# Gated cross-attention with RMS norm: another order for the last outer product and for the norms of the last four tiles

## The chip, the cores and the metric

The kernel runs on one core of a Trainium2 chip. The core has five engines that run side by side, each with its own list of instructions in a fixed order: TensorE (PE, matmuls into PSUM; PEld is its loading of weights), VectorE (DVE), ScalarE (ACT), GpSimd (POOL) and SyncE (SP), which here only issues DMAs. Engines wait for each other by semaphores. The metric is the time of one execution in microseconds (us), measured on the device.

## The reference

Eight batches of 1024 rows (`hidden_states`, the input x), 1024 wide, attend to a memory of 64 rows of 512 per batch (the context), which is projected first. All is fp32.

```
memory_proj = einsum('bme,de->bmd', memory, W_mem)
scores = einsum('bnd,bmd->bnm', hidden_states, memory_proj) / sqrt(D)
attn = softmax(scores)
memory_context = einsum('bnm,bmd->bnd', attn, memory_proj)
gate_input = concatenate([hidden_states, memory_context], -1)
gate = sigmoid(einsum('bnf,df->bnd', gate_input, W_gate) + b_gate)
fused = hidden_states + gate * memory_context
out = fused * rsqrt(mean(fused**2) + 1e-6) * norm_w
```

## The kernel before

**Tiles and stages.** A setup projects the memory and multiplies the projection with the second half of the gate's weights, so that what remains per row is x times the first half of `W_gate` (1024 x 1024) plus attention times that product. Then 16 "quads" follow, each of 4 tiles of 128 rows (`QT` = 512, `NQ` = 16). The large product of a quad is done by a two-level Strassen-Winograd scheme: seven outer products (`ORDER`: 1, 6, 7, 5, 4, 2, 3), each of which is made of seven inner products named A, B, C, D, A, E, F, of 128 x 256 results in PSUM banks `kA` to `kF`. The last but one call of `outer_product` takes 8.16 us (its first matmul at 944.12 us, that of the next call at 952.28).

**One outer product.** `product` issues two matmuls (four records in the trace) and calls `step`, which first runs everything that falls due at this slot. VectorE forms the running sums `u2`, `u3`, `u4` from B, C and D (lines with `u<-u,kB` and so on). GpSimd adds them into the blocks of the output (`pre`, three additions of 128x256). VectorE adds the finished banks (`fin`). GpSimd also forms the left sums of the next outer product (`inner_s`, tiles `l`), in two parts of two additions.

**The last four outer products of a quad** also complete blocks of the output: they have an `ext`, and between the second product into A and product E they issue attention's part, sixteen records of 64-row matmuls. Half of them go into two banks `pc` (attention times projected memory, for two tiles of 128x512), and the other half add attention's share of the gate to `kA`, `kF`, `kE` and `kD`. The pairs go in the order `pc`/A, `pc`/F, then, in the second `pc` bank, `pc`/E, `pc`/D. A bank may be written only after VectorE has read what it held: two `pc` banks take turns, and `kD` must have been read by `u<-u,kD`.

**After an outer product with `ext`**: `sigmoid` on ScalarE (in place, tile `gate`), `gated` on VectorE (times `pc`), then the residual x, the mean of squares, the norm and the store. In the last quad (`q` = `NQ`-1) x has been loaded into tile `xl` (`load_last`), and VectorE adds it (`last_gated`, line 714 and on); ScalarE squares with an accumulator (line 724) and folds in the other half's sum (line 727) or takes the square root (`last_root`, line 736); VectorE takes the reciprocal and scales by it and by `nw_sb`, the norm's weights (`last_norm`, lines 745 and 749); SP stores 128x512 at a time. Outer product 4 completes tiles 2 and 3 ("row 1"), outer product 3 tiles 0 and 1 ("row 0"), the first halves of both having been done before. In a row, `d` is the odd tile and `c` the even one; `d` goes first. ScalarE must load a table of functions when it goes from sigmoid to square root (`sqrt_table`, line 756, does so ahead of the need).

**Order.** Every instruction is pinned to its place in the program, so an engine runs its list in the order of the calls. What falls due is set by slots: `at(slot + n, fn, ...)`. For the last two outer products before:

```
            when = (4, 5, 7, 9, 11, 12) if o == 4 else (2, 4, 5, 6, 7, 8)
            at(slot + when[0], last_root, d)
            at(slot + when[1], last_root, c)
            for w_, (t, h_) in zip(when[2:], ((d, 0), (d, 1), (c, 0), (c, 1))):
                at(slot + w_, last_norm, t, h_)
```

Of the kernel before, what the change touches and what calls it, by code (L numbers as in the profile page):

```python
# [9 lines left out]
AF = mybir.ActivationFunctionType  # L10
ALU = mybir.AluOpType
# [4 lines left out]
P = 128  # L16
# [4 lines left out]
def tile_gated_cross_attention_rmsnorm(  # L21
# [42 lines left out]
    nc = tc.nc  # L64
    B, N, D = x.shape
    M, E = mem.shape[1:]
    QT = 4 * P
    QPB = N // QT
    NQ = B * QPB
# [3 lines left out]
    H = 512  # L73
    C = 256
# [14 lines left out]
    pin = tc.keep_in_program_order  # L89

    def mm(o, lhsT, rhs, start, stop):
        pin(nc.tensor.matmul(o, lhsT, rhs, start=start, stop=stop, skip_group_check=True))  # L92

    def tt(eng, o, a, b, op):
        pin(eng.tensor_tensor(o, a, b, op))  # L95

    def load(o, i):
        pin(nc.sync.dma_start(o, i))

    def t4k(pool, shape, tag, name):  # L100
        return pool.tile(shape, F32, tag=tag, name=name)
# [34 lines left out]
    for k in range(KD):  # L136
        t = t4k(*((gpool, [P, D], "gate") if k < 7 else (apool, [P, D], "s4")), f"w2_{k}")
# [8 lines left out]
    nw_sb = const.tile([P, D], F32, name="nw_sb")  # L146
# [10 lines left out]
    R11, R21, R12, R22, T4, T1, T2 = range(7)  # L157
# [14 lines left out]
    def w_op(o, s):  # L172
        if s >= T4:
            return inner_t[o][:, s - T4, :, :]
        k, n = {R11: (0, 0), R21: (1, 0), R12: (0, 1), R22: (1, 1)}[s]
        return outer_b[o][:, 2 * k : 2 * k + 2, n * C : (n + 1) * C]
# [158 lines left out]
    A, S, L2, O = {}, {}, {}, {}  # L335
    sTs, attns, attnTs, scs, mps, mgs = {}, {}, {}, {}, {}, {}
    def where(q, t=0):
        return q // QPB, (q % QPB) * QT + t * P
# [30 lines left out]
    def left(q, o):  # L369

        return {
            1: lambda: A[q, 0, 0],
            2: lambda: A[q, 0, 1],
            3: lambda: S[q, 4],
            4: lambda: A[q, 1, 1],
            5: lambda: S[q, 1],
            6: lambda: S[q, 2],
            7: lambda: S[q, 3],
        }[o]()

    def quarters(l):
        return l[:, 0:2, 0:P], l[:, 2:4, 0:P], l[:, 0:2, P:], l[:, 2:4, P:]
# [214 lines left out]
    def at(slot, fn, *args):  # L597
        due.setdefault(slot, []).append(lambda: fn(*args))

    def mid(key, fn, *args):  # L600
        beside.setdefault(key, []).append(lambda: fn(*args))
# [47 lines left out]
    slot = 0  # L649

    def step():
        nonlocal slot
        for fn in due.pop(slot, ()):
            fn()

    def gated(q, t, h, pc):
        g = O[q, t][:, h * H : (h + 1) * H]
        tt(nc.vector, g, g, pc, ALU.mult)
# [46 lines left out]
    xl, halves = {}, {}  # L705
# [8 lines left out]
    def last_gated(t, h, pc):  # L714
        q = NQ - 1
        gated(q, t, h, pc)
        cols = slice(h * H, (h + 1) * H)
        g = O[q, t][:, cols]
        tt(nc.vector, g, g, xl[t][:, cols], ALU.add)
        if t not in halves:  # L720
            halves[t] = t4k(small, [P, 3], f"halves{t}", f"halves{t}"), h
        ss, first = halves[t]
        junk = t4k(small, [P, H], "junk", f"junk_{t}_{h}")
        pin(nc.scalar.activation(junk, g, AF.Square, accum_out=ss[:, h : h + 1]))
        if h == first:
            pin(
                nc.scalar.activation(
                    ss[:, 2:3], ss[:, h : h + 1], AF.Identity, bias=eps_sb, scale=1.0 / D
                )
            )  # L730

    def last_root(t):
        ss, first = halves[t]
        h = 1 - first
        pin(
            nc.scalar.activation(
                ss[:, 2:3], ss[:, h : h + 1], AF.Sqrt, bias=ss[:, 2:3], scale=1.0 / D
            )
        )

    def last_norm(t, h):
        b, n0 = where(NQ - 1, t)
        rstd = halves[t][0][:, 2:3]
        if h == 0:
            pin(nc.vector.reciprocal(rstd, rstd))
        cols = slice(h * H, (h + 1) * H)
        g = O[NQ - 1, t][:, cols]
        pin(
            nc.vector.scalar_tensor_tensor(g, g, rstd, nw_sb[:, cols], ALU.mult, ALU.mult)  # L749
        )  # L750
        load(out[b, n0 : n0 + P, cols], g)

    def sqrt_table():

        t = t4k(small, [P, 1], "warm", "warm")
        pin(nc.scalar.activation(t, eps_sb, AF.Sqrt))

    def outer_product(q, o, ext):

        nonlocal slot, banks  # L760
        l11, l12, l21, l22 = quarters(left(q, o))
        s1, s2, s3, s4 = (L2[q, o][:, i, :, :] for i in range(4))
        kb = {}

        def product(name, tag, lhsT, s, start=True):
            nonlocal slot
            step()
            if name not in kb:
                kb[name] = ps.tile([P, C], F32, tag=banks[tag], name=f"k{name}{q}_{o}")
            for k in range(2):  # L770
                mm(kb[name], lhsT[:, k, :], w_op(o, s)[:, k, :], start and k == 0, k == 1)
            slot += 1
# [24 lines left out]
        def pre(n, u):  # L797

            for dst, src in sums:
                if src is not None:  # L800
                    tt(nc.gpsimd, dst[n], src[n], u, ALU.add)

        def fin(n, name, u):
            for dst, src in sums:
                if src is not None:
                    tt(nc.vector, dst[n], (src if u is None else dst)[n], kb[name], ALU.add)
                elif u is not None:
                    tt(nc.vector, dst[n], u, kb[name], ALU.add)
                else:
                    pin(nc.scalar.copy(dst[n], kb[name]))  # L810

        ut = t4k(rot, [P, 4, C], "u", f"u{q}_{o}")
        p1, u2, u3, u4 = (ut[:, i, :] for i in range(4))
# [8 lines left out]
        product("D", 3, s1, T1)  # L822
        tt(nc.vector, u4, u2, kb["D"], ALU.add)
        pre(1, u4)
        product("A", 0, l12, R21, False)
        pcs = []
        if ext:
            row, h, g = ext
# [3 lines left out]
            for r, names in ((0, ("A", "F")), (1, ("E", "D"))):  # L832
                pc = ps_ctx.tile([P, H], F32, tag="ctx", name=f"pc{q}_{o}_{r}")
                for n in range(2):
                    cols = slice(h * H + n * C, h * H + (n + 1) * C)
# [14 lines left out]
                pcs.append(pc)  # L850
        for fn in beside.pop((q, o), ()):
            fn()
        fin(0, "A", None)
        fin(3, "D", u3)
        product("E", 4, l22, T4, not ext)
        fin(2, "E", u3)
        if ext:
            sigmoid(q, 2 * row + 1, h)
            last = q + 1 == NQ
            if last:  # L860
                at(slot + 2, last_gated, 2 * row + 1, h, pcs[1])
            else:
                at(slot + 1, gated, q, 2 * row + 1, h, pcs[1])
        product("F", 1, s4, R22, not ext)
        fin(1, "F", u4)
        if ext:
            sigmoid(q, 2 * row, h)
            if last:
                at(slot + 3, last_gated, 2 * row, h, pcs[0])
            else:  # L870
                at(slot + 2, gated, q, 2 * row, h, pcs[0])
        if o in (4, 3) and q + 1 == NQ:
            c, d = 2 * ext[0], 2 * ext[0] + 1
            if o == 3:
                sqrt_table()
            when = (4, 5, 7, 9, 11, 12) if o == 4 else (2, 4, 5, 6, 7, 8)
            at(slot + when[0], last_root, d)
            at(slot + when[1], last_root, c)
            for w_, (t, h_) in zip(when[2:], ((d, 0), (d, 1), (c, 0), (c, 1))):
                at(slot + w_, last_norm, t, h_)  # L880
        elif o in (4, 3):

            row = ext[0]
            c, d = 2 * row, 2 * row + 1
            for t in (d, c):
                at(slot + 5, residual, q, t)
            if row == 0:
                when = (17, 18, 23, 29, None, None)
            else:
                when = (17, 18, 23, 25, 29, 32)  # L890
            at(slot + when[0], square, q, c)
            at(slot + when[1], square, q, d)
            for w_, (t, h_) in zip(when[2:], ((c, 0), (c, 1), (d, 0), (d, 1))):
                if w_ is None:
                    mid((q + 1, 4), norm, q, t, h_)
                else:
                    at(slot + w_, norm, q, t, h_)
# [3 lines left out]
    for q in range(NQ):  # L901
        plan(q)
        for o, ext in ORDER:
            outer_product(q, o, ext)
    while due:
        slot = min(due)
# [27 lines left out]
```

## Time and profile before

| what | value |
|---|---|
| median of 4 runs | 972.51 us (972.19 to 972.57) |
| the profiled execution, its own time | 972.55 us |
| its span, first to last instruction | 970.7 us |
| granted TensorE clock, mean | 0.997 |
| TensorE busy | 959.2 us (99%) |
| VectorE busy | 818.7 us (84%) |
| GpSimd busy | 760.3 us (78%) |
| ScalarE busy | 328.6 us (34%) |
| end of the last matmul on the chain | 960.86 us |

In the order of time a line has the start in us, the duration in us, the engine, the line of the kernel, the operation, what is written and what is read, the shapes and the number of instructions merged; in brackets the idle time ahead of it and what ended that. The first duration of a merged line is the sum from first start to last end. Line 92 is the helper of all matmuls, line 95 that of all two-operand steps, line 98 that of all DMAs on SP's queue, so the names of tiles tell them apart. In the chain of work that ended last a line has start, duration and the engine whose work filled that time.

In the last 60 us the outer product of block 2 runs from 944.1 us, that of block 3 (the last) from 952.3 us.

### The profile page before, as it was taken

Reading aid. Unit: us, or ns where it says so; the run is one execution under the profiler, and the core shown is the slowest. Engines: PE = TensorE matmul, PEld = TensorE weight load, DVE = VectorE, ACT = ScalarE, POOL = GpSimd, SP = SyncE. Lnnn points to the kernel's source line nnn. Section 1 sums busy time; section 2 is a strip of 40 time slices with the busy share of each in tenths; the row PEclk is TensorE's granted clock in tenths of the full one; section 3 lists DMA queues with packets and bytes.
Section 4 is the critical chain, followed back from the end, with each engine's and each line's share of the span. In section 5 each row is a group of like instructions: output and inputs, shape, how many; then the busy total and the mean of one; then the engine's idle time right before and its main releaser. Section 6 shows DMA issues by size and latency. Waiting matters only on the chain.

```text
span 970.7 us, 14402 instructions
## 1 busy us (share of the span) xinstructions
PE 959.2 (99%) x4986; PEld 774.7 (80%) x4986; DVE 818.7 (84%) x1482; ACT 328.6 (34%) x604; POOL 760.3 (78%) x889
## 2 busy tenths in 40 slices
PE   9999999999999999999999999999999999999995
PEld 8646888788888888788888888888888878888884
DVE  6989879879797988979797988979797978979787
ACT  2000234161423334152433324152333425152345
POOL 4997878778786968878786978878687878878692
PEclk9999999999999999999999999999999999999998
DMA  9956673472919374482918365381918465391712
GB/s 375 273 142 160 101 133 96 117 166 73 177 66 167 107 134 103 107 176 64 186 65 158 104 137 114 93 190 53 197 67 147 114 129 122 87 196 48 189 68 86
DMA packets 70919, 128.32 MB, mean 132 GB/s; under 512 B 12352, under 2 KB 49216, under 8 KB 70592
## 3 DMA queue, kind: packets, MB, share of 16 engines
q1 hardware_dynamic: 61520, 93.34, 37.0%
q0 software_dynamic: 9184, 33.56, 18.9%
q8 instruction: 39, 0.64, 0.3%
q10 hardware_dynamic: 144, 0.52, 0.2%
q14 instruction: 32, 0.26, 0.1%
HBM read 87.56 MB, written 41.68 MB: 133 GB/s over the span
## 4 chain that ended last, share of the span: by engine, by line
PE 97%; DVE 1%; DMA 1%; ACT 0%; issue 0%; DVEq 0%
PE kA L92 20%; PE pc L92 12%; PE kE L92 11%; PE kD L92 10%; PE kF L92 10%; PE kC L92 10%; PE kB L92 10%; PE psT L92 6%; PE pg L92 5%; PE pm L92 3%; DMA memq<-in_mem 1%; PE sc L417 0%; PE pa L443 0%; DVE gate L749 0%; DVE it L95 0%
## 5 line engine op out<-in xcount | busy, mean ns | idle before, releaser
L95 POOL TENSOR_TENSOR gate<-gate,u 128x256 f32<-128x256 f32 x336 | 287.5, 887 | 107.3 <-DVE u L95 107.3
L662 ACT ACTIVATE gate<-gate 128x512 f32<-128x512 f32 x128 | 80.5, 631 | 305.5 <-DVE gate L95 304.8
L349 DVE STREAM_TRANSPOSE a<-xq 128x512 f32<-128x512 f32 x128 | 137.8, 1098 | 3.6 <-POOL w L95 3.6
L95 POOL TENSOR_TENSOR l<-a 128x256 f32<-128x256 f32 x128 | 122.4, 956 | 21.6 <-PE kA L92 21.6
L92 PE MATMUL pc<-mg,attnT 64*128 64x256 f32 x512 | 127.5, 389 | 0.0
L92 PE MATMUL kB<-it,l 128*128 128x256 f32 x448 | 115.1, 379 | 0.3 <-DVE gate L95 0.3
L92 PE MATMUL kD<-it,l 128*128 128x256 f32 x448 | 115.0, 379 | 0.0
L92 PEld LDWEIGHTS pc<-mg,attnT 64*128 64x128 f32 x512 | 90.6, 186 | 29.9 <-issue 21.2
L691 DVE SCALAR_TENSOR_TENSOR gate<-gate,ss,nw_sb 128x512 f32<-128x512 f32 x120 | 110.0, 926 | 1.1
L95 POOL TENSOR_TENSOR l<-s 128x256 f32<-128x256 f32 x96 | 77.8, 810 | 37.2 <-PE kF L92 30.4
L92 PE MATMUL kA<-w,a 128*128 128x256 f32 x384 | 98.6, 379 | 0.0
L92 PEld LDWEIGHTS kB<-it,l 128*128 128x128 f32 x448 | 85.1, 190 | 12.1 <-DVE gate L95 0.7
L92 PEld LDWEIGHTS kD<-it,l 128*128 128x128 f32 x448 | 85.2, 190 | 11.5
L95 DVE TENSOR_TENSOR gate<-gate,pc 128x512 f32<-128x512 f32 x128 | 86.6, 677 | 0.4 <-ACT gate L662 0.4
L95 DVE TENSOR_TENSOR gate<-gate,kE 128x256 f32<-128x256 f32 x112 | 45.4, 417 | 47.5 <-PE kE L92 41.8
L92 PEld LDWEIGHTS kA<-w,a 128*128 128x128 f32 x384 | 71.8, 190 | 9.5 <-issue 0.5
L815 ACT COPY u<-kA 128x256 f32<-128x256 f32 x112 | 40.5, 361 | 109.9 <-PE kA L92 106.0
L92 PE MATMUL kE<-it,a 128*128 128x256 f32 x256 | 69.0, 392 | 0.0
L676 ACT ACTIVATE junk<-gate 128x1024 f32<-128x1024 f32 x60 | 63.5, 1058 | 12.5 <-DMA gate<-in_x 11.5
L92 PE MATMUL kA<-t,s 128*128 128x256 f32 x256 | 65.8, 380 | 0.0
L92 PE MATMUL kC<-w,l 128*128 128x256 f32 x256 | 65.7, 379 | 0.0
L92 PE MATMUL kF<-w,l 128*128 128x256 f32 x256 | 65.7, 379 | 0.0
(140 smaller groups left out, 2039.3 us busy)
## 6 DMA issues: line engine op xcount, KB each, us to landing
xq<-in_x SPq DMA_DIRECT2D x64, 512.0 KB, 10.2
gate<-in_x POOLq DMA_DIRECT2D x60, 512.0 KB, 8.0
out<-gate SPq DMA_DIRECT2D x60, 512.0 KB, 2.6
w<-in_w_gate_t SPq DMA_DIRECT2D x8, 512.0 KB, 10.0
w<-in_w_gate_t SPq DMA_DIRECT2D x2, 2048.0 KB, 16.6
mg<-mgd SPq DMA_DIRECT2D x16, 256.0 KB, 3.7
mpd<-mpT SPq DMA_DIRECT2D x4, 512.0 KB, 7.1
mgd<-mpq SPq DMA_DIRECT2D x16, 128.0 KB, 3.8
```

The lines of the kernel that those rows point to most:

```text
L92: pin(nc.tensor.matmul(o, lhsT, rhs, start=start, stop=stop, skip_group_check=True))
L95: pin(eng.tensor_tensor(o, a, b, op))
L349: nc.vector.transpose(A[key][:, :, r * P : (r + 1) * P], chunks(xq[q][:, 4 * t : 4 * t + 4, :], KD)[:, half * KH : (half + 1) * KH],)
L662: pin(nc.scalar.activation(g, g, AF.Sigmoid))
L676: nc.scalar.activation(junk, O[q, t], AF.Square, accum_out=ss[:, t % 2 : t % 2 + 1])
L691: nc.vector.scalar_tensor_tensor(g[:, cols], g[:, cols], rstd[:, t % 2 : t % 2 + 1], nw_sb[:, cols], ALU.mult, ALU.mult,)
L815: pin(nc.scalar.copy(p1, kb["A"]))
```

## The change

It concerns the last quad alone, from the end of outer product 4 on.

- **Order of the last outer product.** The second product into A goes behind E: A, B, C, D, attention's part, E, A, F. A new function, `finish`, holds everything from there on.
- **The last tiles by quarters.** In `finish` the sigmoids are four of 128x256, each issued after the sum that completes its quarter (D, E, A, F), in place of two of 128x512. `gated` for tile 1 is issued between E's and A's sums; for tile 0 it is done in two quarters. GpSimd adds x to tile 1, VectorE to tile 0.
- **Half of the norms weighed by GpSimd.** For the half of a tile that was completed first, GpSimd multiplies by `nw_sb` into `xl` (`weigh`), ahead of the mean being known. When the mean is there, one scaling by the reciprocal remains (`last_scale`): on ScalarE for tiles 3, 2 and 0, on VectorE for tile 1. The other half goes as before (`last_norm`). A reciprocal is now taken in the half that is normalised first.
- **Row 1's places.** Its two `weigh` are issued at the end of outer product 4, ahead of the left sums of outer product 3 in GpSimd's list; the norms stand at slots +7 and +9 and ScalarE's scalings at +8 and +10.

```diff
@@ last_gated: the square becomes a function of its own, last_square
@@ last_norm
-        if h == 0:
+        if h != halves[t][1]:
             pin(nc.vector.reciprocal(rstd, rstd))
@@
+    def weigh(t, h):
+        cols = slice(h * H, (h + 1) * H)
+        tt(nc.gpsimd, xl[t][:, cols], O[NQ - 1, t][:, cols], nw_sb[:, cols], ALU.mult)
+
+    def last_scale(t, h, on_act):
+        b, n0 = where(NQ - 1, t)
+        rstd = halves[t][0][:, 2:3]
+        cols = slice(h * H, (h + 1) * H)
+        g = xl[t][:, cols]
+        if on_act:
+            pin(nc.scalar.activation(g, g, AF.Copy, scale=rstd))
+        else:
+            pin(nc.vector.tensor_scalar(g, g, rstd, None, ALU.mult))
+        load(out[b, n0 : n0 + P, cols], g)
@@
+    def finish(ext, pcs, fin, product, a2, e, f, u3, u4):
+        ...
+        fin(3, "D", u3)
+        sigmoid_quarter(d, 1)
+        product("E", 4, *e, False)
+        fin(2, "E", u3)
+        sigmoid_quarter(d, 0)
+        product("A", 0, *a2, False)
+        gated(q, d, h, pcs[1])
+        fin(0, "A", None)
+        sigmoid_quarter(c, 0)
+        add_x(nc.gpsimd, d)
+        weigh(c, 1 - h)
+        product("F", 1, *f, False)
+        fin(1, "F", u4)
+        sigmoid_quarter(c, 1)
+        sqrt_table()
+        for n in range(2):
+            g = O[q, c][:, cols(n)]
+            tt(nc.vector, g, g, pcs[0][:, n * C : (n + 1) * C], ALU.mult)
+        add_x(nc.vector, c)
+        last_square(d, h)
+        last_root(d)
+        last_square(c, h)
+        last_root(c)
+        last_norm(d, h)
+        last_scale(d, 1 - h, False)
+        last_norm(c, h)
+        last_scale(c, 1 - h, True)
@@ outer_product
-        product("A", 0, l12, R21, False)
+        tail = o == 3 and q + 1 == NQ
+        if tail:
+            weigh(2 * ext[0] + 1, 0)
+        else:
+            product("A", 0, l12, R21, False)
@@ (after attention's part)
+        if tail:
+            finish(ext, pcs, fin, product, (l12, R21), (l22, T4), (s4, R22), u3, u4)
+            return
@@
-        if o in (4, 3) and q + 1 == NQ:
+        if o == 4 and q + 1 == NQ:
             c, d = 2 * ext[0], 2 * ext[0] + 1
-            if o == 3:
-                sqrt_table()
-            when = (4, 5, 7, 9, 11, 12) if o == 4 else (2, 4, 5, 6, 7, 8)
-            at(slot + when[0], last_root, d)
-            at(slot + when[1], last_root, c)
-            for w_, (t, h_) in zip(when[2:], ((d, 0), (d, 1), (c, 0), (c, 1))):
-                at(slot + w_, last_norm, t, h_)
+            at(slot + 4, last_root, d)
+            at(slot + 5, last_root, c)
+            for i, t in enumerate((d, c)):
+                at(slot, weigh, t, 1)
+                at(slot + 7 + 2 * i, last_norm, t, 0)
+                at(slot + 8 + 2 * i, last_scale, t, 1, True)
```

More of the change, by code (lines that the diff above doesn't have):

```diff
@@ L719, in last_gated, with last_square @@
         tt(nc.vector, g, g, xl[t][:, cols], ALU.add)
+        last_square(t, h)
+    def last_square(t, h):
+        cols = slice(h * H, (h + 1) * H)
+        g = O[NQ - 1, t][:, cols]
         if t not in halves:
@@ L751, in last_norm @@
         load(out[b, n0 : n0 + P, cols], g)
+    def weigh(t, h):
[4 more added lines that the diff above has]
+        rstd = halves[t][0][:, 2:3]
+        cols = slice(h * H, (h + 1) * H)
+        g = xl[t][:, cols]
[4 more added lines that the diff above has]
+        load(out[b, n0 : n0 + P, cols], g)
     def sqrt_table():
@@ L756, in sqrt_table, with cols, sigmoid_quarter, add_x @@
         pin(nc.scalar.activation(t, eps_sb, AF.Sqrt))
+    def finish(ext, pcs, fin, product, a2, e, f, u3, u4):
+        row, h, _ = ext
+        c, d = 2 * row, 2 * row + 1
+        q = NQ - 1
+        def cols(n):
+            return slice(h * H + n * C, h * H + (n + 1) * C)
+        def sigmoid_quarter(t, n):
+            g = O[q, t][:, cols(n)]
+            pin(nc.scalar.activation(g, g, AF.Sigmoid))
+        def add_x(eng, t):
+            g = O[q, t][:, h * H : (h + 1) * H]
+            tt(eng, g, g, xl[t][:, h * H : (h + 1) * H], ALU.add)
+        fin(3, "D", u3)
[25 more added lines that the diff above has]
+        last_scale(c, 1 - h, True)
     def outer_product(q, o, ext):
```

## The prediction

> **What bounds the kernel now.** I read the busy table first, then the chain of work that ended last, then the order of time from 943 us on, where every instruction that the diff touches lies.
>
> ```profile
> PE 959.2 (99%) x4986; PEld 774.7 (80%) x4986; DVE 818.7 (84%) x1482; ACT 328.6 (34%) x604; POOL 760.3 (78%) x889
> PE 97%; DVE 1%; DMA 1%; ACT 0%; issue 0%; DVEq 0%
> ```
> TensorE is full from start to end. Its last product ends at 960.86 us and the span is 970.7 us, so two things count: whether TensorE gets later, and what the last 9.84 us become. The chain there:
> ```profile
> 959.98 0.88 PE kF L92 x4
> 960.95 0.43 DVE gate L95
> 961.41 0.63 ACT gate L662
> 962.05 1.28 ACT L756
> 963.55 0.62 ACT junk L724 x2
> 964.72 1.42 DVE gate L749 x2
> 966.24 0.75 DVE gate L749
> ```
> Last product, its sum, last sigmoid, the load of the square root's table, squares, norms. The order of time shows what VectorE does just before, beside the last outer product:
> ```profile
> 955.08 0.41 DVE L95 TENSOR_TENSOR u<-u,kB 128x256 f32<-128x256 f32 x1
> 955.41 0.74 DVE L749 SCALAR_TENSOR_TENSOR gate<-gate,halves,nw_sb 128x512 f32<-128x512 f32 x1
> 956.07 0.41 DVE L95 TENSOR_TENSOR u<-u,kC 128x256 f32<-128x256 f32 x1
> 956.40 0.68 DVE L95 TENSOR_TENSOR gate<-gate,pc 128x512 f32<-128x512 f32 x1
> 957.12 0.72 DVE L95 TENSOR_TENSOR gate<-gate,xl 128x512 f32<-128x512 f32 x1
> 957.76 0.41 DVE L95 TENSOR_TENSOR u<-u,kD 128x256 f32<-128x256 f32 x1
> ```
> and TensorE beside it:
> ```profile
> 955.74 1.03 PE L92 MATMUL kA<-w,s 128*128 128x256 f32 x4
> 956.69 0.48 PE L92 MATMUL pc<-mg,attnT 64*128 64x256 f32 x1
> 958.23 0.48 PE L92 MATMUL kD<-mg,attnT 64*128 64x256 f32 x1
> 958.85 1.13 PE L92 MATMUL kE<-it,s 128*128 128x256 f32 x4
> 959.82 1.03 PE L92 MATMUL kF<-w,l 128*128 128x256 f32 x4
> ```
> The sum from kD ends at 958.17, and the first matmul that adds attention's part to kD starts at 958.23: TensorE waits for VectorE to have read bank D. In the outer product before it the attention part takes 1.92 us from its first matmul (948.53) to E (950.45); here 2.16 us (956.69 to 958.85). So 0.24 us of this wait shows already, and the rest of VectorE's lateness is hidden by the second product into A at 955.74.
>
> **The change part by part.**
>
> *A goes behind E.* TensorE's work is the same, but its cover is gone. From one four-matmul product to the next takes 0.865 us (954.87 to 955.74), from A to attention's part 0.95 us (955.74 to 956.69). So attention's part now asks to start at 954.87 + 0.95 = 955.82, and without waits E would start 1.92 us later, at 957.74. It has two waits. Its second half (`pc`, row 1) needs the bank that VectorE's `gate<-gate,pc` of the product before releases: in the outer product of block 4 the second half began at 940.60, just behind the end of that read at 940.55. The last matmul needs the sum from kD.
>
> VectorE cannot be earlier: its `u<-u,kB` starts at 955.08, when product B is ready, as before. Behind it stood one norm (0.66 us to the next start), now a reciprocal (0.18 us, 958.10 to 958.28) and one norm. So `gate<-gate,pc` runs at 956.58 to 957.26 and `u<-u,kD` ends at 958.17 + 0.18 = 958.35. Attention's second half would come at 955.82 + 0.97 = 956.79 and waits until 957.32; its last matmul waits until 958.41, and E starts 0.62 us later (as 958.23 to 958.85): 959.03. Then A and F: F starts at 959.03 + 0.97 + 0.865 = 960.87, against 959.82 before. **TensorE ends 1.05 us later.** That is 0.865 us of lost cover and 0.18 us of reciprocal. Lower end 0.87 us, if the reciprocal costs nothing; upper end 1.5 us, if the add of x slows from 0.72 us to the 1.19 us that it took at 937.87.
>
> *Row 1's norms.* On VectorE two 128x512 norms go (0.66 us each). One stood in the stretch above, where another norm takes its place; the other two steps stood behind 958.17, where VectorE now waits for TensorE anyway. Worth nothing. ScalarE gets two scalings of 128x512 (nearest row: its 128x512 activation, 0.631 us) at about 954.4 and 956.3; it had 0.79 and 1.63 us of idle time before the squares there. Worth nothing; the square of row 0 ends near 959.2, before the first quarter's sigmoid at 959.7. The four stores of row 1 on SP's queue come earlier than 953.86, 956.18, 959.06 and 960.38 or at the same time, and none of them waits for a tile that is later than its successor.
>
> *GpSimd's weighing of row 1.* Two 128x512 multiplications are put before the left sums of the last outer product, which start at 944.78. GpSimd's 128x512 rows are 1.27 us alone to 2.27 us beside other work; in this window VectorE's only work with two operands in SBUF is the two adds of x, so I take 1.5 and 1.4 us. Then the two left sums (0.73 and 0.9) end near 949.4, and the three sums for block 2 (0.72 to 0.85 each) end near 950.2, 951.0 and 951.8. VectorE asks for them at 950.67, 951.69 and 952.55. Hidden, with 0.5 to 0.8 us to spare; the other left sums end by 953.4, and product C asks for them at 954.01.
>
> The Trainium skill's GPSIMD Engine Reference, section Engine selection, speaks against this: it says that GpSimd is the wrong engine for elementwise work on two tensors, about twice as slow as VectorE. The rows here agree (1.27 to 2.27 us against 0.69 us for VectorE's add of x at 961-963 us), but by its rule moving all four weighings of 128x512 to VectorE would be right, and the sum above says that only their place counts, since GpSimd was idle for 4.85 us before 956.56.
>
> *The tail.* Times from here: kD's part is ready 0.14 us after its last matmul (950.53 to 950.67), so its sum starts at 959.24 and the first quarter's sigmoid at 959.7. E's sum starts 1.24 us after E (950.45 to 951.69): 960.27. The second quarter's sigmoid, 128x256, is bounded by ScalarE's copy and exponential of that size, 0.36 and 0.417 us; I take 0.417, since both work on SBUF: 960.72 to 961.14. VectorE's `gated` follows at 961.18, A's sum at 961.84, F's at 962.18 (F itself is ready at 960.87 + 1.13 = 962.00). Sigmoids of tile 0: 962.28, and 962.63 to 963.05. The table load starts at 963.06, against 962.05: 1.05 + 0.19 for F's sum behind `gated`, less 0.21 for the narrower sigmoid. **+1.01 us.** From there to the first square 1.41 us as before (962.05 to 963.46): 964.47.
>
> That square reads what GpSimd has added: the three sums end at 959.8 (0.17 us later than 959.62), then a weighing, the add of x (not before `gated` ends at 961.9) and the second weighing. At 1.3 to 1.5 us each: 961.3, 963.4, 964.9. At 2.27 us: 962.1, 964.3, 966.6. The square needs the add by 964.4, the last scaling the weighing by 967.2. Hidden at both ends. VectorE's own steps for tile 0 (0.41, 0.41, 0.69 to 1.19) end before 964.8; the second square starts at 965.4.
>
> Norms: reciprocal 965.53, norm 965.73. Then one VectorE scaling, a kind that the trace doesn't have: from 0.33 us (a 256-wide step's distance) to 0.66 us (a norm's). I take 0.66, the row of the same width. Reciprocal of tile 0 at 967.05, its norm at 967.24; ScalarE's scaling runs beside it, 967.25 to 967.9. Before, the last norm started at 966.90 (0.78 us ahead of its store's issue at 967.68, as below). So ScalarE's help takes one norm off the end, and the last results are only 0.35 us later.
>
> The Trainium skill's VectorE: DVE Perf Modes, section The perf-mode tier table, gives an fp32 `tensor_scalar` in SBUF twice the rate of `tensor_tensor`; with its 1.23 us at 2048 elements I estimate 0.42 us here, which would make the sum 0.3 us smaller. No row shows one.
>
> *The drain.* Stores of 256 KB, issues 0.33 us long:
> ```profile
> 965.50 0.33 SPq L98 DMA_DIRECT2D out<-gate  x1
> 967.02 0.33 SPq L98 DMA_DIRECT2D out<-gate  x1
> 967.68 0.33 SPq L98 DMA_DIRECT2D out<-gate  x1
> ```
> and, in the table by stretches (last column GB/s), the writing itself:
> ```profile
> 968.00:968.50 0.50, 0.00 (x0) 0.00 (x0) 0.00 (x0) 0.00 (x0) 0.00 (x0) 0.50 1.04 389
> ```
> Bytes flow 0.81 us after an issue (965.50 to 966.31) at 385 GB/s, 0.68 us a store. A norm's issue comes 0.78 us after its start (964.72 to 965.50). After: third store issued at 968.02, fourth at 968.37, side by side. Their bytes flow from 968.83 for 1.36 us to 970.19, where before the fourth's ended at 967.68 + 0.81 + 0.68 = 969.17. **The end moves by 1.02 us**: 0.67 by the rule of rate if the scaling takes 0.33. The step that ScalarE saved is given back here, because the two stores now come together.
>
> Sum: the profiled run took 972.55 us (span 970.7 and 1.85 around it), 0.04 above the median of 972.51. 972.51 + 1.0 = **973.5 us**, 0.1% more. A measurement of this kernel tells about 0.2% (1.95 us) from no change, so this is no change.
>
> **Rivals.**
> 1. *Gain.* TensorE is held up less than I think (`u<-u,kD` read by 957.4 and not 958.35). Then F ends with before, and the tail gains 0.2 us by the narrower sigmoid and up to 0.35 by the shorter norms: 972.0 to 972.4. Against it: five VectorE steps of 0.33 to 0.72 us stand in line behind product B, and B can't be earlier.
> 2. *GpSimd's add of x ends the wait for the square.* Its sums at 1.27 us and both 512-wide steps at 2.27 give 965.1, 0.6 us too late: 974.1. For it: 1.27 us rows at 924.84. Against: VectorE has mostly operands in PSUM there.
> 3. *Slower.* The weighings of row 1 make the sums for block 2 late, at 950.67 to 952.55. VectorE works in order, so its whole line to `u<-u,kD` shifts, and TensorE, without cover now, with it. At 2.27 us per weighing and 0.9 to 1.02 per sum GpSimd ends at 954.2, 1.7 us after VectorE's asking: 973.5 + 1.7 = 975.2. It decides beyond 0.2% from about 0.95 us of lateness, GpSimd ending at 953.5. Against: its rows from 944 to 950 are 0.72 to 0.85.
>
> **How the numbers follow.** Forecast 0.70, with 973.0 to 974.1 its own range; rival 1 0.12; rival 2 0.09; rival 3 0.06, of which 0.05 beyond 0.2%; others 0.03, of which 0.02 faster by more than 0.2%. Range 972.2 to 974.7: it takes rivals 1 in part and 2 whole. Faster 0.02, within 0.92, slower 0.06.
>
> **What the profile after would show.** Right: a gap in TensorE of about 0.5 us ahead of the third `pc` pair and again ahead of kD; F ending near 961.9; the table load near 963.1; last bytes near 970. Wrong: E starting before 958.5; VectorE's sums of block 2 waiting for GpSimd near 951 us; the first square waiting for GpSimd; a scaling much shorter than 0.6 us (then nearer 973.2).

## The result

The changed kernel takes 973.15 us (median of 33 runs, 972.71 to 973.98), the kernel before 972.22 us (median of 53, 971.82 to 972.88). The ratio is 1.001, with a 95% interval of 1.0005 to 1.0015: slower by 0.9 us or 0.1%, which counts as no change by the bound of 0.2%. The prediction had 973.5 us: 1.0 us on top of 972.51 us, the median of the 4 runs known then, where the median of 53 is 972.22 us.

The profiled execution of the changed kernel took 972.75 us with a span of 971.0 us. It can't be laid directly beside that of before: the first matmul of the last product B, up to which the two programs hardly differ, starts at 952.47 us here and at 953.15 us there, and it starts anywhere from 952.47 to 953.40 us in the profiled executions below. So I count from this matmul ("mark 0"). The 0.98 us by which the span then ends later agrees with the 0.93 us between the medians, so mark 0 itself is not shifted by the change as far as these runs tell. By it the two kernels compare like this (us):

| | last E | last F | load of the square root's table | first square of tile 1 | end of the span |
|---|---|---|---|---|---|
| before | 5.70 | 6.67 | 8.90 | 10.31 | 17.55 |
| after | 5.90 | 7.73 | 9.86 | 11.26 | 18.53 |
| difference | +0.20 | +1.06 | +0.96 | +0.95 | +0.98 |
| predicted | +0.18 | +1.05 | +1.01 | +1.01 | +1.02 |

Of the loss of 0.98 us, 0.96 us is there when the table load begins; from the load to the end both take nearly the same time (8.65 and 8.67 us).

The order of time of the changed kernel, beside the last outer product, answers to the lines that the prediction shows of VectorE and TensorE:

```profile
954.73 0.16 DVE L750 RECIPROCAL halves<-halves 128x1 f32<-128x1 f32 x1
...
954.92 0.75 DVE L754 SCALAR_TENSOR_TENSOR gate<-gate,halves,nw_sb 128x512 f32<-128x512 f32 x1
...
955.59 0.41 DVE L95 TENSOR_TENSOR u<-u,kC 128x256 f32<-128x256 f32 x1
...
955.92 0.68 DVE L95 TENSOR_TENSOR gate<-gate,pc 128x512 f32<-128x512 f32 x1
...
956.64 0.72 DVE L95 TENSOR_TENSOR gate<-gate,xl 128x512 f32<-128x512 f32 x1
...
956.66 0.18 PEld L92 LDWEIGHTS pc<-mg,attnT 64*128 64x128 f32 x1 [0.77 <-DVE gate L95]
...
957.28 0.41 DVE L95 TENSOR_TENSOR u<-u,kD 128x256 f32<-128x256 f32 x1
...
957.74 0.29 PEld L92 LDWEIGHTS kD<-mg,attnT 64*128 64x128 f32 x2 [0.36 <-DVE u L95]
```
TensorE now waits twice, for the read of the older `pc` bank and for the sum from bank D, as predicted: in the kernel before the first wait was hidden by the second product into A.

The chain of work that ended last, of the changed kernel, from product E on (earlier, from 954.40 to 956.61 us, it runs through VectorE's line: the sum from B, the reciprocal, the norm, the sum from C, `gated`):

```profile
958.44 1.07 PE kE L92 x4
...
959.61 0.43 DVE gate L95
...
960.06 0.42 ACT gate L792
...
960.51 1.03 DVE gate L95 x2
...
961.56 0.75 ACT gate L792 x2
...
962.33 1.28 ACT L778
```
What matters is what is absent. Before, the chain went from product F to the table load. Now it leaves TensorE at product E: E's sum, the second sigmoid of tile 1, then two VectorE steps in a row (`gated` and A's sum), the last sigmoids, the load. Neither the moved A nor F is on it. F's sum was ready 1.13 us after F began, at 961.33, and VectorE came to it at 961.45.

So two things limit the end at nearly the same time: TensorE, 1.06 us later, and VectorE's list, in which `gated` of tile 1 stands ahead of F's sum.

One sign that the prediction named for being wrong seems to be there: VectorE's sum from E for block 2 is put down as waiting for GpSimd, where before it waited for TensorE. Before, then after:

```profile
951.69 0.42 DVE L95 TENSOR_TENSOR gate<-gate,kE 128x256 f32<-128x256 f32 x1 [0.60 <-PE kE L92]
...
951.01 0.42 DVE L95 TENSOR_TENSOR gate<-gate,kE 128x256 f32<-128x256 f32 x1 [0.60 <-POOL gate L95]
```
The wait has not grown (0.60 us both times), and the sum starts 1.24 us after product E both times (950.45 and 949.77 us). GpSimd's sum that it needs is the second of three, which take 2.08 us from 948.89 us on, so it ended near 950.3 us. Nothing is lost there.

The experiments take the two limits apart.

### The profile page after: what moved, and what is told of

Its sections match the earlier page's. It is cut to its first block, busy times and chain, and to the rows that moved or that the text cites. A ratio compares the mean times of both kernels' runs of the same rounds, so it can differ in the third digit from the quotient of the medians.

```text
span 971.0 us, 14412 instructions
## 1 busy us (share of the span) xinstructions
PE 959.5 (99%) x4986; PEld 774.9 (80%) x4986; DVE 813.9 (84%) x1479; ACT 330.8 (34%) x609; POOL 767.7 (79%) x894
## 4 chain that ended last, share of the span: by engine, by line
PE 98%; DVE 1%; ACT 0%; issue 0%; DVEq 0%; ACTq 0%
PE kA L92 20%; PE pc L92 12%; PE kE L92 11%; PE kD L92 10%; PE kB L92 10%; PE kC L92 10%; PE kF L92 10%; PE psT L92 6%; PE pg L92 5%; PE pm L92 3%; PE pz L92 0%; PE pa L443 0%; PE sc L417 0%; DVE gate L95 0%; PE pt L196 0%
```

## The experiments

Each was timed in 5 rounds beside the kernel before on the same chip. All marks are from one profiled execution each, counted from the last product B.

| run | E | F | table load | end of the span | ratio to before (95%) |
|---|---|---|---|---|---|
| A behind E alone, in the kernel before | 5.71 | 7.54 | 9.77 | 18.50 | 1.0009 (1.0000 to 1.0018) |
| changed, A ahead again | 5.90 | 6.87 | 9.87 | 18.51 | 1.0010 (1.0001 to 1.0019) |
| changed, `gated` behind F's sum | 5.90 | 7.73 | 9.76 | 18.66 | 1.0010 (1.0001 to 1.0019) |
| changed, both | 5.90 | 6.87 | 8.89 | 17.71 | 1.0001 (0.9992 to 1.0010) |
| changed, tile 2's norm later | 5.24 | 7.07 | 9.90 | 18.49 | 1.0011 (1.0002 to 1.0020) |
| changed, VectorE's line lightened, A behind | 4.61 | 6.44 | 9.01 | 17.61 | 0.9999 (0.9991 to 1.0008) |
| changed, VectorE's line lightened, A ahead, `gated` late | 5.48 | 6.44 | 8.46 | 17.27 | 0.9997 (0.9988 to 1.0006) |
| changed, one weighing more on GpSimd | 6.26 | 8.09 | 10.21 | 18.86 | 1.0020 (1.0011 to 1.0029) |
| changed, no scaling of tile 0 by ScalarE | 5.90 | 7.73 | 9.86 | 18.55 | 1.0008 (0.9999 to 1.0017) |
| changed, row 1's norms as before | 5.70 | 7.54 | 10.46 | 19.07 | 1.0013 (1.0005 to 1.0022) |

### The order of A alone, in the kernel before

```diff
-        product("A", 0, l12, R21, False)
+        tail = o == 3 and q + 1 == NQ
+        if not tail:
+            product("A", 0, l12, R21, False)
...
-        fin(0, "A", None)
+        if not tail:
+            fin(0, "A", None)
...
+        if tail:
+            product("A", 0, l12, R21, False)
+            fin(0, "A", None)
         product("F", 1, s4, R22, not ext)
```

> The kernel before, with only the second product into A (and its sum) moved behind E. My working: E at 5.70 us after B as before, since kD's read by VectorE sets it, F at 7.54 and the load at 9.77 (before: 6.67 and 8.90), total +0.87: 973.1. Rival (the tail's other order is what costs, TensorE's order nothing): no change, 972.2.

Measured 972.93 us against 972.08, ratio 1.0009 (1.0000 to 1.0018). E comes at 5.71, where it came before, although the work ahead of it is 0.865 us shorter:

```profile
957.39 0.48 PE L92 MATMUL pc<-mg,attnT 64*128 64x256 f32 x1 [0.17 <-DVE gate L95]
...
958.02 0.41 DVE L95 TENSOR_TENSOR u<-u,kD 128x256 f32<-128x256 f32 x1
...
958.48 0.70 PE L92 MATMUL kD<-mg,attnT 64*128 64x256 f32 x2
...
959.11 1.13 PE L92 MATMUL kE<-it,s 128*128 128x256 f32 x4
...
962.07 0.42 DVE L95 TENSOR_TENSOR gate<-gate,kF 128x256 f32<-128x256 f32 x1 [0.18 <-PE kF L92]
```
VectorE's sum from D ends at 958.43, and the matmul into kD starts at 958.48. F and the load are 0.87 us later than before. Here VectorE waits for F's part (last line), so TensorE's lateness goes to the end in full: the product that moved had been cover for VectorE's line.

### A ahead again, in the changed kernel

```diff
         if tail:
             weigh(2 * ext[0] + 1, 0)
-        else:
-            product("A", 0, l12, R21, False)
+        product("A", 0, l12, R21, False)
...
-        product("A", 0, *a2, False)
         gated(q, d, h, pcs[1])
```

> The changed kernel with the second product into A put back ahead of attention's part; all else as changed. Marks are us after the first matmul of the last product B (changed kernel: E 5.90, F 7.73, table load 9.86). Theory 1 (TensorE's lost cover is the whole loss): F and the load come 0.87 us earlier, total 972.3. Theory 2 (the line that ends is E's sum, second sigmoid, `gated`, A's sum, F's sum on VectorE, and A's place alone doesn't shorten it): E 5.9, F 6.87, but the load stays at 9.8 to 9.9, total 973.1, within 0.1 of the changed kernel.

Measured 972.98 us against 972.08, ratio 1.0010 (1.0001 to 1.0019). F is 0.86 us earlier and nothing else is:

```profile
959.36 1.03 PE L92 MATMUL kF<-w,l 128*128 128x256 f32 x4
...
960.53 0.69 DVE L95 TENSOR_TENSOR gate<-gate,pc 128x512 f32<-128x512 f32 x1 [0.48 <-ACT gate L792]
...
961.14 0.41 DVE L95 TENSOR_TENSOR gate<-gate,kA 128x256 f32<-128x256 f32 x1
...
961.47 0.42 DVE L95 TENSOR_TENSOR gate<-gate,kF 128x256 f32<-128x256 f32 x1
```
F's part was ready at 960.49 (1.13 us after F began), but VectorE stands at `gated`, which waits for a sigmoid, and takes F's sum only at 961.47. Theory 2 holds: A's place alone is not the loss of the changed kernel.

### `gated` behind F's sum, alone and together with A ahead

```diff
-        gated(q, d, h, pcs[1])
         fin(0, "A", None)
         sigmoid_quarter(c, 0)
-        add_x(nc.gpsimd, d)
-        weigh(c, 1 - h)
         product("F", 1, *f, False)
         fin(1, "F", u4)
+        gated(q, d, h, pcs[1])
+        add_x(nc.gpsimd, d)
+        weigh(c, 1 - h)
         sigmoid_quarter(c, 1)
```

> The changed kernel, A behind E, with only `gated` of tile 1 and GpSimd's add of x issued behind F's sum. This is the fourth corner beside the changed kernel, the one with A ahead (load 9.87) and the one with both (8.89). If each of the two limits is enough to hold the end: F's sum is taken when F is ready, 1.13 us after 7.73, the load at 9.75, 0.1 us below the changed kernel, and the first square waits for GpSimd, so the total is within 0.1 us of it, 973.1. If `gated`'s place alone is the loss: load 8.9, total 972.3.

Alone, with A behind E: 973.4 us against 972.16, ratio 1.0010 (1.0001 to 1.0019). The load comes at 9.76, 0.10 us earlier than in the changed kernel, as expected. The time is 0.3 us above the 973.1 us expected, and the span ends at 18.66, 0.13 us later than in the changed kernel; the ratio to the kernel before is the same.

> As the one before, and `gated` of tile 1 with GpSimd's add of x issued behind F's sum. Theory 2: F's sum is then ready and taken at 8.0, the load at 8.9, total 0.85 us below the changed kernel, 972.3. Theory 1: as the one before it, no further gain from `gated`'s place.

Together: 972.26 us against 972.08, ratio 1.0001 (0.9992 to 1.0010), load at 8.89. Its chain ends on TensorE again:

```profile
958.76 1.06 PE kE L92 x4
...
959.82 0.88 PE kF L92 x4
...
960.79 0.43 DVE gate L95
...
961.25 0.42 ACT gate L792
...
961.68 1.28 ACT L778
```
The four corners of this square have the load at 9.86, 9.87, 9.76 and 8.89. Undoing either of the two moves alone gives back nearly nothing, because the other one still holds the end, and undoing both gives back 0.97 us. With both undone the load is where it was before (8.89 and 8.90). The span still ends 0.16 us later (17.71 and 17.55), 0.1 us of it because the first square now waits for GpSimd's add of x: it starts 1.51 us behind the load, before 1.41 us. The times don't tell this from nothing.

### Tile 2's norm two slots later

```diff
-                at(slot + 7 + 2 * i, last_norm, t, 0)
-                at(slot + 8 + 2 * i, last_scale, t, 1, True)
+                at(slot + 7 + 4 * i, last_norm, t, 0)
+                at(slot + 8 + 4 * i, last_scale, t, 1, True)
```

> The changed kernel with tile 2's reciprocal and norm (and its scaling) two slots later, out of VectorE's line between the sums from B and D. If VectorE's line sets E: E at 5.05 to 5.1 us after B (5.90 in the changed kernel), F 6.9, load 9.05, total 0.8 us less, 972.35. If TensorE's own work sets it: no change.

Measured 973.15 us against 972.08, ratio 1.0011 (1.0002 to 1.0020): no gain. E did come earlier, by 0.66 us (5.24), so VectorE's line sets it. That is less than the 0.84 us taken out of the line. The sum from C, which reads the sum from B, now follows it directly and starts 0.52 us behind it (954.94 and 955.46), where a step of that size that reads nothing of the one before starts 0.33 us behind it. But the load stayed at 9.90:

```profile
958.47 1.26 POOL L95 TENSOR_TENSOR xl<-gate,nw_sb 128x512 f32<-128x512 f32 x1
...
958.95 1.32 DVE L754 SCALAR_TENSOR_TENSOR gate<-gate,halves,nw_sb 128x512 f32<-128x512 f32 x1
...
960.20 0.41 DVE L95 TENSOR_TENSOR gate<-gate,kE 128x256 f32<-128x256 f32 x1
...
960.64 0.42 ACT L792 ACTIVATE gate<-gate 128x256 f32<-128x256 f32 x1 [1.35 <-DVE gate L95]
```
The norm now runs beside GpSimd's new weighing, takes 1.32 us in place of 0.75, and delays E's sum, which was ready at 959.49 (1.24 us after E), to 960.20. My expectation went by TensorE's marks and left out that the norm lands on the line from E's sum.

### VectorE's line lightened

With A behind E, the add of x to tile 0 and tile 2's norm are issued between the sum from D and D's part:

```diff
         if tail:
+            g = O[q, 0][:, :H]
+            tt(nc.vector, g, g, xl[0][:, :H], ALU.add)
+            last_square(0, 0)
+            last_norm(2, 0)
             weigh(2 * ext[0] + 1, 0)
...
-            if last:
+            if last and o == 2:
+                at(slot + 3, gated, q, 2 * row, h, pcs[0])
+            elif last:
                 at(slot + 3, last_gated, 2 * row, h, pcs[0])
...
-                at(slot + 7 + 2 * i, last_norm, t, 0)
-                at(slot + 8 + 2 * i, last_scale, t, 1, True)
+                if t == d:
+                    at(slot + 7, last_norm, t, 0)
+                at(slot + 8 + 4 * i, last_scale, t, 1, True)
```

> The changed kernel, A still behind E. VectorE's line between the sums from B and D holds only the sum from C and `gated` of tile 0's other half; that half's add of x and tile 2's reciprocal and norm are issued behind the sum from D and ahead of D's part. If VectorE's line set E in the changed kernel, E comes at 4.6 us after B (5.90 there), F at 6.45, E's sum isn't delayed (the norm stands ahead of D's part), the table load at 8.6 (9.86), and the end 1.25 us below the changed kernel and 0.3 below the kernel before: 971.9. If a rest of the loss has another cause, the load stays above 8.9.

Measured 972.15 us against 972.20, ratio 0.9999 (0.9991 to 1.0008). E came at 4.61, F at 6.44: TensorE hardly waits any more in this stretch: without waits the prediction's working puts E at 957.74 us, 4.59 after mark 0. The load came at 9.01 and not 8.6:

```profile
956.21 1.19 DVE L95 TENSOR_TENSOR gate<-gate,xl 128x512 f32<-128x512 f32 x1
...
957.50 1.03 DVE L754 SCALAR_TENSOR_TENSOR gate<-gate,halves,nw_sb 128x512 f32<-128x512 f32 x1
...
958.79 0.41 DVE L95 TENSOR_TENSOR gate<-gate,kE 128x256 f32<-128x256 f32 x1
```
Both moved steps were slowed (0.72 to 1.19 and 0.75 to 1.03 us), and E's sum, ready at 958.34, came at 958.79. With A ahead, `gated` behind F's sum and tile 2's norm two slots later, which with A ahead puts it between the sum from D and D's part (the edits of the two sections before this one, together):

> The changed kernel with A ahead of attention's part, `gated` of tile 1 behind F's sum, and tile 2's norm behind the sum from D. E at 5.46 us after B, F at 6.43, load at 8.43; the first square 1.5 us behind the load, since GpSimd's add of x then ends last; 0.35 us below the kernel before: 971.8. If `gated`'s place and VectorE's line had no effect, it equals the changed kernel.

Measured 971.86 us against 972.20, ratio 0.9997 (0.9988 to 1.0006). The marks are those expected (E 5.48, F 6.44, load 8.46, first square at 9.97), and the span ends 0.28 us earlier after mark 0 than before the change. The time itself can't tell 0.3 us from nothing: this kernel has the lowest median of all, but it is not shown to be faster than the kernel before.

### One weighing more on GpSimd

```diff
             for i, t in enumerate((d, c)):
                 at(slot, weigh, t, 1)
+                if t == d:
+                    at(slot, weigh, t, 1)
```

> The changed kernel with one of GpSimd's two weighings of row 1 done twice (the same values again), 1.3 to 1.5 us more ahead of the left sums and of the sums for block 2. In the changed kernel these sums ended 0.4, 0.7 and 0.9 us before VectorE could take them. So they come 0.4 to 1.1 us late, VectorE's line shifts by 0.4 to 0.6 us, E at 6.3 to 6.5 after B, total +0.5 against the changed kernel. If the weighing is hidden with more to spare: no change.

Measured 973.97 us against 972.20, ratio 1.0020 (1.0011 to 1.0029). E at 6.26, 0.36 us later, and the load 0.35 us later:

```profile
944.37 4.22 POOL L95 TENSOR_TENSOR xl<-gate,nw_sb 128x512 f32<-128x512 f32 x3
...
951.24 0.42 DVE L95 TENSOR_TENSOR gate<-gate,kD 128x256 f32<-128x256 f32 x1 [1.44 <-POOL gate L95]
...
951.92 0.42 DVE L95 TENSOR_TENSOR gate<-gate,kE 128x256 f32<-128x256 f32 x1 [0.27 <-POOL gate L95]
...
952.61 0.42 DVE L95 TENSOR_TENSOR gate<-gate,kF 128x256 f32<-128x256 f32 x1 [0.26 <-POOL gate L95]
```
Now VectorE waits for GpSimd three times. So the two weighings of row 1 are hidden in the changed kernel, but a third one, 1.2 us more (4.22 against 3.00 us), is past the slack. This is the mechanism of the prediction's third rival, brought about by hand. Only 0.33 us of the loss against the changed kernel stands in the marks of the profiled execution, which was one of the shorter (973.46 us). The runs scatter more than the others' (973.2 to 975.7 us): the two longest had a granted clock of 0.995, the four shortest 0.998. Why is open, and how much of the 973.97 us is the third weighing's is not shown.

### No scaling of tile 0 by ScalarE

```diff
         last_norm(c, h)
-        last_scale(c, 1 - h, True)
+        last_norm(c, 1 - h)
```
GpSimd's weighing of that half is left out with it.

> The changed kernel with tile 0's first half normalised by VectorE at the very end, as before the change, and not weighed by GpSimd and scaled by ScalarE. If ScalarE's help is given back because the last two stores come together: last issue 0.2 us later than in the changed kernel, the end 0.0 to 0.2 us earlier. If ScalarE's help is worth the norm it takes off VectorE: the end 0.4 to 0.7 us later.

Measured 973.01 us against 972.20, ratio 1.0008 (0.9999 to 1.0017); the span ends at 18.55 after mark 0, in the changed kernel at 18.53. The stores, issued on SP's queue, in the changed kernel:

```profile
967.10 0.33 SPq L98 DMA_DIRECT2D out<-gate  x1
...
967.52 0.40 SPq L98 DMA_DIRECT2D out<-xl  x1
```
The last issue is 15.05 after mark 0 and the end 3.48 us behind it; in the kernel before it was 14.53 and 3.02. Without ScalarE's scaling the last issue comes 0.2 us later than in the changed kernel (about 15.3, an estimate, since the trace merges the last two issues: 0.99 us from 967.18 us on), and the end is the same within 0.02 us. ScalarE takes one norm off VectorE's end, and the gain is given back, as the prediction's drain had it. But it is not the last two stores alone that run one behind the other. In the changed kernel and in this one the first of the four stores is issued at 13.41 after mark 0 (965.88 and 965.96 us), the bytes begin at 14.2, and they flow at about 360 to 400 GB/s without a gap until 17.0. So here the end follows from the first store's issue and the bytes of all four; in the kernel before there is a gap ahead of the last two stores (189 GB/s from 967.75 to 968.00 us).

### Row 1's norms as before

```diff
-            at(slot + 4, last_root, d)
-            at(slot + 5, last_root, c)
-            for i, t in enumerate((d, c)):
-                at(slot, weigh, t, 1)
-                at(slot + 7 + 2 * i, last_norm, t, 0)
-                at(slot + 8 + 2 * i, last_scale, t, 1, True)
+            when = (4, 5, 7, 9, 11, 12)
+            ...
```

> The changed kernel with row 1's norms as before the change (four norms on VectorE, no weighing by GpSimd and no scaling by ScalarE for row 1). If moving row 1's norms is worth nothing, as I worked out: E 0.2 us earlier (5.70, no reciprocal in VectorE's line), which tile 2's norm ahead of E's sum takes back as it did where it stood there; load 9.7 to 9.9, total 973.0 to 973.2. If it relieves VectorE on the path: load and total 0.5 us later or more.

Measured 973.6 us against 972.16, ratio 1.0013 (1.0005 to 1.0022); the load came at 10.46, 0.60 us later than in the changed kernel:

```profile
959.34 1.33 DVE L754 SCALAR_TENSOR_TENSOR gate<-gate,halves,nw_sb 128x512 f32<-128x512 f32 x1
...
960.59 0.41 DVE L95 TENSOR_TENSOR gate<-gate,kE 128x256 f32<-128x256 f32 x1
...
960.92 0.74 DVE L754 SCALAR_TENSOR_TENSOR gate<-gate,halves,nw_sb 128x512 f32<-128x512 f32 x1
...
961.59 0.67 DVE L95 TENSOR_TENSOR gate<-gate,pc 128x512 f32<-128x512 f32 x1
```
My expectation counted the norm ahead of E's sum and not the second one, which stands ahead of `gated`, on the line that ends the changed kernel. So row 1's part of the change is worth 0.5 to 0.6 us inside the new order; in the kernel before, F's sum still had to wait 0.27 us for TensorE behind these norms, so they delayed nothing that the end waited for.

## Why the prediction was right

- *TensorE later by 1.05 us: right (1.06), by 0.87 us of cover and 0.2 us of reciprocal.* A behind E alone moved F by 0.87 us at an unchanged E, and with row 1's norms as before E went back to 5.70.
- *The line from E's sum through `gated` to F's sum: right, and more than the prediction made of it.* It gave this line 0.19 us on top of TensorE. In truth it is a second limit of nearly the same size: with TensorE's loss undone the end didn't move. Its sum, TensorE's 1.05 us with small things added and taken off, was right as a number and incomplete as a cause.
- *GpSimd's weighing hidden: right.* Row 1's two took 3.00 us, where 2.9 was worked out. The sums for block 2 ended in time, by an estimate 0.4, 0.7 and 0.9 us before VectorE took them (three equal parts of 2.08 us from 948.89 us on, taken at 949.99, 951.01 and 951.88 us), and 1.2 us more was too much, as the third weighing showed. In the tail the weighing and the add took 1.26, 1.27 and 1.26 us, and ScalarE didn't wait for them.
- *Row 1's norms worth nothing: right for the sum, wrong as a price of the part* (above: 0.5 to 0.6 us inside the new order).
- *The scaling on VectorE: too dear in the prediction.* It took 0.66 us from the row of a norm, and set an estimate of 0.42 us from the Trainium skill's VectorE: DVE Perf Modes, section The perf-mode tier table, beside it. Measured:

```profile
965.73 0.48 DVE L772 TENSOR_SCALAR xl<-xl,halves 128x512 f32<-128x512 f32 x1
```
  A scaling much shorter than 0.6 us was among the prediction's signs of being wrong, and the estimate from the page was nearer. The sum 0.3 us smaller, 973.2, that the prediction derived from it does not follow, though, and its nearness to the 973.15 measured is luck: the end still came 0.98 us later after mark 0. The 0.35 us between 973.5 and 973.15 lies mostly in the base, 972.51 against 972.22.
- *VectorE's add of x to tile 0: outside the bounds.* I allowed 0.69 to 1.19 us; beside GpSimd's work it took 1.52 us (last section). It ended at 964.32, 0.35 us before ScalarE squared that tile, so it cost nothing.
- *The drain: right in kind, incomplete.* The stores run one behind the other, and ScalarE's help is lost there. The prediction counted the last two stores alone; counted so with the scaling as measured (0.40 us to the next start), its own figures would move the end by only about 0.8 us. All four run without a gap, and this holds in its own figures too: the first norm at 965.73 issues its store at 966.51, bytes flow from 967.32, and four times 0.68 us end at 970.04, 0.87 us later than before and 0.15 us short of its 970.19. So that it came out at 1.02 us is partly luck: the price of the scaling, too high, stood in for a bound that was left out.
- *Rival 1 (gain)* did not come, for the reason given against it. What it needed was made by hand in the lightened kernels, and E then came 0.2 to 1.1 us earlier than before.
- *Rivals 2 and 3* did not come: GpSimd's add of x ended at 962.55, 1.18 us before the first square, and row 1's sums ended in time. The 2.27 us per step of 128x512 that they were worked out with is a mean over rows, and the longest single row of the kernel before took 2.95 us; in the tail the steps took 1.26 and 1.27 us.

## What to carry to other kernels

A product that seems movable may be the cover under which another engine finishes its reads; before moving it, ask which wait it hides, and take that wait's length as the price. Where an in-order list holds a step that waits (here `gated`, for a sigmoid) ahead of one that is ready, that step is a limit of its own, and undoing one of two limits of the same size shows nothing; undo both. And a saving at the very end is worth only as much as the last transfers let through.

## What the runs showed of the hardware

VectorE's steps with two operands in SBUF and GpSimd's two-operand work slow each other down. The add of x, 128x512, took 0.69 us in the kernel that leaves out GpSimd's last weighing, and in the changed kernel, beside the weighing:

```profile
962.51 1.26 POOL L95 TENSOR_TENSOR xl<-gate,nw_sb 128x512 f32<-128x512 f32 x1
...
962.80 1.52 DVE L95 TENSOR_TENSOR gate<-gate,xl 128x512 f32<-128x512 f32 x1
```
The norm went from 0.75 to 1.33 us in the same way, and GpSimd's own weighing from 1.26 to 1.72 us where the two engines overlapped otherwise (in the kernels with `gated` behind F's sum). Which of the two loses differs. The add of x at 956.64 us (shown in the section on the result) kept 0.72 us beside GpSimd's sums, and there these took longer, 2.54 us against 2.08 us for three where VectorE read PSUM:

```profile
948.89 2.08 POOL L95 TENSOR_TENSOR gate<-gate,u 128x256 f32<-128x256 f32 x3
...
956.08 2.54 POOL L95 TENSOR_TENSOR gate<-gate,u 128x256 f32<-128x256 f32 x3 [3.75 <-DVE u L95]
```
In these rows the step that started first kept its time: GpSimd's weighing (962.51) ahead of VectorE's add (962.80), and VectorE's add (956.64) ahead of the second of GpSimd's sums (956.76). No experiment was made on this. Steps with one operand in PSUM kept their time: `gate<-gate,pc` took 0.68 us at 955.92, beside GpSimd's sums from 956.08 on, and 0.69 us at 960.51, where GpSimd stood idle. The Trainium skill's GPSIMD Engine Reference, section Specifications, says that the two engines share their way into SBUF, and that they get in each other's way where a VectorE instruction has two inputs in SBUF. The rows agree that both lose where a VectorE step has two inputs in SBUF. So in a tail the engine to which work is moved can slow the one that it is to relieve.
